# Output projection in seven block products per pair of sequences, with the sums of y made in the heads and kept in memory

## The chip, the cores and the metric

The kernel runs on one core of a Trainium2 chip. The metric is the device time of one execution in microseconds (us). One execution was also profiled, instruction by instruction. Engines: PE is TensorE, PEld its weight loads, DVE is VectorE, ACT is ScalarE, POOL is GpSimd, and SP is SyncE, which here issues nearly all DMA transfers, in program order.

## The reference

Four sequences of 512 tokens, 512 features; 16 heads of 128; a router over 64 experts. All in float32.

```python
def reference(x, slope_rate, w_qkv, w_gate, w_out, norm_w, router_weight, router_bias, expert_bias):
    xn = layernorm(x)
    # lightning attention on xn: per head a decayed causal attention
    q, k, v = split(silu(xn @ w_qkv.T))              # 16 heads of 128
    out = decayed_causal_attention(q, k, v, slope_rate)
    var = mean(out * out, -1)                        # over all 16 heads
    out = norm_w * (out * rsqrt(var + 1e-6))
    gate = sigmoid(xn @ w_gate.T)
    s = (gate * out) @ w_out.T                       # the output projection
    # router: top 8 of 64 by softmax
    scores = softmax(xn @ router_weight.T + router_bias)
    topk_w, topk_idx = top_k(scores, 8)
    f = xn * sum(topk_w) + sum(topk_w * expert_bias[topk_idx])
    return x + s * silu(f)
```

## The kernel before

PE multiplies float32 through a split: each operand becomes a high part (a cast to float32r, made on ScalarE by `split_hi`, L99) and a low part (the operand minus the high part, made by `split_lo`, L102, on VectorE or GpSimd). A product is then three passes (`PASSES`, L27): high by high, high by low and low by high.

The four sequences form two pairs (`PB` = 2, p = 0 and 1), the 16 heads eight groups of two (`GH`, `NG`). The kernel has three stages. The order of all instructions is written out by hand; Tile adds only the waits.

1. *Preparation and v* (to 186 us): layer norm, transposes, the router's logits, and v for all tokens, which goes to device memory.

2. *Heads* (to 863 us). The list `todo` has 24 units per pair: for each group a gate unit (`gate_unit`) and two units for q and k (`qk_unit`). Each unit is computed by `unit` (L484) in the Winograd form of a 2 by 2 block product: seven products instead of eight (`PRODUCTS`, L39), here with two sequences as one side's blocks and two weight matrices as the other's. A product is six matmuls of 128 x 512. Its result leaves its PSUM bank through an `add` on VectorE, or a copy on ScalarE. Between the products stand the lists `after[0]` to `after[6]`: the work of other steps that is issued after that product. There are the splits of the next unit's weights (on GpSimd), the attention of the head whose q and k were ready before (`attention`: scores in `after[1]`, states in `after[3]`, `attend` in `after[6]`), and in pair 0 the router's selection (`route_steps`). A gate unit has the attention of the group before's second head, the first q and k unit has none, the second has that of the first head. `attend` (L690) multiplies by the norm's weight and the gate and stores y, one tile of 128 x 512 per sequence and head (its features by the tokens), to `y_d`.

3. *Output projection* (from 863 us). `steps` goes over the four sequences and the 16 heads: 64 steps. `ahead` loads y (`load_y`) up to six steps ahead and splits it (`split_y`: high part on ScalarE, low part on VectorE) up to three ahead; in the first sequence it also loads w_o and splits it (`split_wo`, low part on GpSimd). A step is `o_head`: four token tiles by three passes, 12 matmuls with y as the weights of the array and 512 columns of w_o streamed, summed over 16 heads in four PSUM banks. At head 15 `finish` (L791) multiplies by the root mean square and by the gate of the experts, adds x and stores. Between the steps stand the last head's attention (`last_steps`), the sums of squares, and the experts' part (`ffn`, `silu_gate`). The last three heads of the last sequence are taken tile by tile, so that the finishing of a tile lies beside the next one's matmuls.

The last unit holds the start of stage 3:

```python
if i == len(todo) - 1:
    ahead(0, 2, 0)                       # loads of two y
    def more():
        ...
        ahead(0, 4, 1)                   # first split
    after[3].append(more)
    after[4].append(lambda: ahead(0, 4, 2))   # second split
    after[5].append(lambda: load_eb(op))
    after[6].append(lambda: ahead(0, 6, 2))
```

SBUF is handed out by pools. A tile with `bufs=n` shares n buffers with the others of its tag: the next tile waits until all that use the old one, DMA transfers too, are done.

Of the kernel before, what the change touches and what calls it, by code (L numbers as in the profile page):

```python
# [50 lines left out]
def kernel(  # L51
# [50 lines left out]
    def split_lo(eng, lo, src, hi):  # L102
# [31 lines left out]
    }  # L134
    y_d = {
        (b, h): dram.tile([P, N], F32, tag=f"y{b}_{h}", name=f"y_{b}_{h}")
        for b in range(B) for h in range(NH)
    }

# [47 lines left out]
    NX = 3  # L187
# [27 lines left out]
    def load_x(stage, b, t):  # L215
        xt = stage.tile([P, F], F32, tag="x", name=f"x_{b}_{t}")
        nc.sync.dma_start(out=xt, in_=x[tok(b, t), :])
        xts[b, t] = xt
# [470 lines left out]

    def attend(b, h, attp, psum=(ps_o, "o")):  # L690
# [7 lines left out]
        y = attp.tile([P, N], F32, tag="y", name=f"y_{b}_{h}")  # L698
        nc.vector.scalar_tensor_tensor(y, po, nw[:, h : h + 1], gts[s], ALU.mult, ALU.mult)  # L699
        nc.sync.dma_start(out=y_d[s], in_=y)  # L700
# [30 lines left out]
    def load_eb(outp):  # L731
        ebs.append(outp.tile([P, F], F32, tag="woin", name="raw_eb"))
        nc.sync.dma_start(out=ebs[0][0:E, :], in_=expert_b)
        nc.sync.dma_start(out=ebs[0][E : 2 * E, :], in_=expert_b)
# [12 lines left out]
    def ffn(b, t, outp):  # L747
        u = outp.tile([P, F], F32, tag="u", name=f"u_{b}_{t}")
        normalise(u, xts[b, t], b, t)
        pu = ps_sc.tile([P, F], F32, tag="sc", name=f"pu_{b}_{t}")  # L750
        for i in range(2):
            nc.tensor.matmul(pu, wT[b][:, t, :], ebs[0][:, i, :], start=(i == 0), stop=(i == 1))  # L752
        gates[b, t] = u, pu
# [7 lines left out]
    op = late = None  # L761
    wos = {}

    def load_y(b, h, op):
        y = op.tile([P, N], F32, tag="yin", name=f"yin_{b}_{h}")
        nc.sync.dma_start(out=y, in_=y_d[b, h])
        return y

    def split_y(b, h, op, y):
        yr = op.tile([P, 2, N], F32R, tag="yr", name=f"yr_{b}_{h}")  # L770
# [4 lines left out]
    def load_wo(h, op):  # L775
        w = op.tile([P, F], F32, tag="woin", name=f"woin_{h}")
        nc.sync.dma_start(out=w, in_=w_o[h // GH][:, h % GH, :])
        return w


    def split_wo(h, w):
        pool_, tag = (op, f"wr{h}") if h < 4 else (xa, f"x{h - 4}") if h < 4 + NX else (late, f"wr{h}")
        wr = pool_.tile([P, 2, F], F32R, tag=tag, name=f"wr_{h}", bufs=1)
        split_hi(wr[:, 0], w)
        split_lo(nc.gpsimd, wr[:, 1], w, wr[:, 0])
        wos[h] = wr
# [4 lines left out]
    def finish(b, t, ps, c=slice(None)):  # L791
        u, xt = gates[b, t][:, c], xts[b, t][:, c]
        last = b == B - 1
        nc.vector.scalar_tensor_tensor(u, ps[:, c], rms[b][:, t : t + 1], u, ALU.mult, ALU.mult)  # L794
        (nc.vector if last else nc.gpsimd).tensor_tensor(u, u, xt, ALU.add)  # L795

        def store():
            (nc.scalar if last and t % 2 else nc.sync).dma_start(out=out[tok(b, t), c], in_=u)
        if last:
            store()  # L800
        else:
            stores.append(store)


    def o_head(pos, h, yr, t, c=slice(None), stops=(NH - 1,)):
        for n, (wi, yi) in enumerate(PASSES):
            nc.tensor.matmul(  # L807
                pos[t][:, c], yr[:, yi, bass.ts(t, P)], wos[h][:, wi, c],
                start=(h == 0 and n == 0), stop=(h in stops and n == len(PASSES) - 1),
                skip_group_check=c != slice(None),  # L810
            )
# [184 lines left out]
    xc = op2 = None  # L996
    xc_stack = ExitStack()
    steps = [(b, h) for b in range(B) for h in range(NH)]
    parts, ys, ow = [], [], []
# [3 lines left out]
    def ahead(i, loads, splits):  # L1003
        nonlocal nload, nsplit
        while nload < min(i + loads, len(steps)):
            b, h = steps[nload]
            from_ = op if nload < 2 else op2
            ys.append(load_y(b, h, from_))
            if b == 0:
                ow.append(load_wo(h, from_))  # L1010
            nload += 1
        while nsplit < min(i + splits, len(steps)):
            b, h = steps[nsplit]
            from_ = op if nsplit < 2 else op2
            parts.append(split_y(b, h, from_, ys.pop(0)))
            if b == 0:
                split_wo(h, ow.pop(0))
# [9 lines left out]
    for i, (p, kind, n, w) in enumerate(todo):  # L1027
# [18 lines left out]
        if nu - len(XN) + NX <= i < nu:  # L1046
# [5 lines left out]
            load_block(1, m)  # L1052
        if i == nu - 1:
            for m in range(NX):
                def again(m=m):
                    block(1, len(XN) - NX + m, xa, m)
                    load_block(1, len(XN) - NX + m)
                after[m].append(again)
        if i == nu:
            xb_stack.close()  # L1060
            op = left(o_stack, "o", 2)
        if i == len(todo) - 1:
            ahead(0, 2, 0)


            def more():
                nonlocal op2
                xc_stack.close()
                op2 = left(o_stack, "o2", 4)
                ahead(0, 4, 1)  # L1070
            after[3].append(more)
            after[4].append(lambda: ahead(0, 4, 2))
            after[5].append(lambda: load_eb(op))
# [22 lines left out]
    pos = {}  # L1096
    for f in later:
        f()
    for i, (b, h) in enumerate(steps):
        last = b == B - 1  # L1100
        if i == len(last_steps):
            ha_stack.close()
            hw_stack.close()
            late = right(late_stack, "late", 5)

        if h < NH - 1:
            ahead(i, 6, 3)
            while stores:
                stores.pop(0)()
        if h == 0:  # L1110
            for t in range(NT):
                pos[t] = ps_mm.tile([P, F], F32, tag="mm", name=f"po_{b}_{t}")
        if not last or h < NH - TAIL:
            yr = parts.pop(0)
            for t in range(NT):
# [74 lines left out]
```

## Time and profile before

| | |
|---|---|
| time, median of 3 runs | 1060.59 us (1059.93 to 1064.33) |
| the profiled execution's own time | 1060.44 us |
| its span, first to last instruction | 1058.6 us |
| granted TensorE clock | 0.999 |
| PE busy from 0 to 863 us (v and heads) | 860.96 us |
| PE busy from 863 to 1000 us (projection) | 137.00 us |
| VectorE busy, 0 to 863 and 863 to 900 us | 419.91 and 22.04 us |
| GpSimd busy, 0 to 863 and 863 to 900 us | 613.77 and 25.56 us |
| DMA, whole execution | 143.09 MB, 135 GB/s |
| DMA share and rate, 863 to 900 us | 0.66, 220 GB/s |

How to read it: the page of the profile gives busy time by engine, the chain of work that ended last, and groups of instructions; a group's line has source line, engine, operation, tiles (written <- read), shape, count, then busy us, mean ns of one, and the idle time of its engine just before, with the work that ended most of it. The timeline lists instructions in order of time, merged where equal ones follow each other. A matmul's own duration includes its way through the array, so matmuls overlap: their price is the interval from start to start. Time is counted from the start of the span.

### The profile page before, as it was taken

How to read it: one execution, taken by the hardware profiler on the slowest of the kernel's cores; microseconds unless marked ns; L12 is line 12 of the kernel's file. 1: busy time of each engine (PE TensorE's matmuls, PEld its weight loads, DVE VectorE, ACT ScalarE, POOL GpSimd, SP SyncE). 2: the span in 40 equal slices, each digit the busy share in tenths (PEclk: the TensorE clock that was granted, in tenths of full speed). 3: DMA queues.
4: the chain of work that ended last, by engine and by line, in shares of the span. 5: the costliest groups of instructions: out<-in, count | busy, mean ns of one | idle time of the engine just before them, and what ended most of it. 6: DMA issues, size and time to landing. Idle time of an engine off the chain costs nothing.

```text
span 1058.6 us, 16166 instructions
## 1 busy us (share of the span) xinstructions
PE 1051.8 (99%) x5771; PEld 910.6 (86%) x5771; DVE 520.8 (49%) x869; ACT 520.5 (49%) x955; POOL 663.6 (63%) x694
## 2 busy tenths in 40 slices
PE   9999999999999999999999999999999999999998
PEld 8888888888888888888888888888888888888886
DVE  6666543355454545444444444444444456745354
ACT  5555555655555555555555555554555543332221
POOL 5888782857777678677785777767867756402020
PEclk9999999999999999999999999999999999999999
DMA  7456737422422233235722242232322546445351
GB/s 245 165 199 245 266 142 238 150 85 86 140 85 95 89 98 114 85 125 174 279 85 66 88 126 85 85 110 83 107 65 86 159 131 217 140 159 173 96 189 50
DMA packets 109872, 143.09 MB, mean 135 GB/s; under 512 B 9680, under 2 KB 58208, under 8 KB 108896
## 3 DMA queue, kind: packets, MB, share of 16 engines
q1 hardware_dynamic: 108752, 141.35, 40.8%
q8 instruction: 46, 0.75, 0.3%
q10 hardware_dynamic: 1040, 0.71, 0.2%
q14 instruction: 34, 0.28, 0.1%
HBM read 93.24 MB, written 50.87 MB: 136 GB/s over the span
## 4 chain that ended last, share of the span: by engine, by line
PE 98%; DVE 1%; DMA 0%; ACT 0%; POOL 0%; issue 0%; SPq 0%; ACTq 0%
PE u_qk L502 29%; PE po L807 16%; PE u_g L502 14%; PE u_v L502 13%; PE o L695 5%; PE sa L658 5%; PE o L697 4%; PE ss L681 4%; PE kt L661 2%; PE d_v L532 2%; PE lg L318 1%; PE pu L752 1%; PE pt L251 1%; DMA x<-in_x_dram 0%; PE ssq L724 0%; ACT w_A_v L100 0%
## 5 line engine op out<-in xcount | busy, mean ns | idle before, releaser
L807 PE MATMUL po<-wr,yr 128*128 128x512 f32 (+1 forms) x777 | 178.7, 388 | 0.9 <-DVE u L794 0.9
L807 PEld LDWEIGHTS po<-wr,yr 128*128 128x128 f32 x777 | 144.4, 188 | 30.4 <-DVE u L794 1.1
L502 PE MATMUL u_qk<-blk_T,ws_qk 128*128 128x512 f32 x576 | 146.9, 395 | 0.0
L707 POOL TENSOR_TENSOR sqs<-sqs,sq 128x512 f32<-128x512 f32 x60 | 77.8, 1296 | 76.3 <-ACT sq L706 76.3
L502 PEld LDWEIGHTS u_qk<-blk_T,ws_qk 128*128 128x128 f32 x576 | 105.8, 188 | 20.2
L103 POOL TENSOR_TENSOR ws_qk<-sum_qk,ws_qk 128x512 fp32r<-128x512 f32 x64 | 82.8, 1295 | 40.6 <-ACT ws_qk L100 39.6
L502 PE MATMUL u_qk<-blk_B,wa_qk 128*128 128x512 f32 x384 | 99.1, 394 | 0.0
L695 PE MATMUL o<-at,vin 128*128 128x128 f32 x512 | 88.4, 275 | 0.0
L502 PEld LDWEIGHTS u_qk<-blk_B,wa_qk 128*128 128x128 f32 x384 | 71.0, 188 | 14.1
L103 DVE TENSOR_TENSOR yr<-yin,yr 128x512 fp32r<-128x512 f32 x64 | 60.6, 960 | 44.3 <-ACT yr L100 44.1
L103 POOL TENSOR_TENSOR ws_g<-sum_g,ws_g 128x512 fp32r<-128x512 f32 x32 | 41.3, 1290 | 59.1 <-ACT ws_g L100 59.1
L695 PEld LDWEIGHTS o<-at,vin 128*128 128x128 f32 x512 | 75.0, 192 | 2.5
L502 PE MATMUL u_g<-blk_T,ws_g 128*128 128x512 f32 x288 | 76.0, 400 | 0.0
L667 ACT ACTIVATE kd<-kt,kdecay 128x384 f32<-128x384 f32 x64 | 37.2, 582 | 77.8 <-PE kt L661 77.8
L699 DVE SCALAR_TENSOR_TENSOR y<-o,nw,gt 128x512 f32<-128x512 f32 x64 | 48.0, 751 | 55.1 <-PE o L697 55.1
L697 PE MATMUL o<-qd,st 128*128 128x128 f32 x384 | 74.3, 275 | 0.0
L706 ACT ACTIVATE sq<-o 128x512 f32<-128x512 f32 x60 | 35.9, 598 | 75.1 <-POOL sqs L707 42.3
L685 DVE SCALAR_TENSOR_TENSOR st<-st,bdecay,ss 128x128 f32<-128x128 f32 x128 | 41.7, 346 | 59.0 <-ACT st L683 56.8
L795 POOL TENSOR_TENSOR u<-u,x 128x512 f32<-128x512 f32 x12 | 17.8, 1517 | 84.0 <-DVE u L794 84.0
L100 ACT CAST yr<-yin 128x512 fp32r<-128x512 f32 x64 | 39.2, 617 | 63.0 <-PE po L807 39.4
L546 ACT ACTIVATE k<-k 128x512 f32<-128x512 f32 x64 | 40.4, 632 | 57.4 <-DVE k L493 57.4
L658 PE MATMUL sa<-q,k 128*128 128x128 f32 x512 | 67.5, 275 | 0.0
(180 smaller groups left out, 2295.7 us busy)
## 6 DMA issues: line engine op xcount, KB each, us to landing
v<-vo_v SPq DMA_DIRECT2D x64, 256.0 KB, 2.7
raw_qk<-in_w_head_dram SPq DMA_DIRECT2D x64, 256.0 KB, 3.7
vin<-v SPq DMA_DIRECT2D x64, 256.0 KB, 3.6
y<-y SPq DMA_DIRECT2D x64, 256.0 KB, 2.1
yin<-y SPq DMA_DIRECT2D x64, 256.0 KB, 2.8
x<-in_x_dram SPq DMA_DIRECT2D x32, 256.0 KB, 4.3
raw_g<-in_w_head_dram SPq DMA_DIRECT2D x32, 256.0 KB, 3.2
raw_v<-in_w_v_dram SPq DMA_DIRECT2D x16, 256.0 KB, 5.9
```

Source lines behind the costliest of these rows:

```text
L100: nc.scalar.copy(hi, src)
L103: eng.tensor_tensor(lo, src, hi.bitcast(F32), ALU.subtract)
L502: nc.tensor.matmul(ps, lhsT, rhs, start=(first and c == 0 and n == 0), stop=(c == KC - 1 and n == len(PASSES) - 1), skip_group_check=not f ...
L546: nc.scalar.activation(dst, src, AF.Silu)
L658: nc.tensor.matmul(pa[:, c], k[:, c], q[:, c], start=True, stop=True)
L681: nc.tensor.matmul(ps[:, c], kd[s][:, c], v_of(b, h, c), start=True, stop=True)
L685: nc.vector.scalar_tensor_tensor(r[:, c], r[:, c - 1], bdecay[:, h : h + 1], ps[:, c], ALU.mult, ALU.add)
L695: nc.tensor.matmul(o, v_of(b, h, c), at[s][:, c], start=True, stop=(c == 0))
L697: nc.tensor.matmul(o, st[s][:, c - 1], qd[s][:, c - 1], start=False, stop=True)
L699: nc.vector.scalar_tensor_tensor(y, po, nw[:, h : h + 1], gts[s], ALU.mult, ALU.mult)
L707: nc.gpsimd.tensor_tensor(sq[b], sq[b], s1, ALU.add)
L807: nc.tensor.matmul(pos[t][:, c], yr[:, yi, bass.ts(t, P)], wos[h][:, wi, c], start=(h == 0 and n == 0), stop=(h in stops and n == len(PASS ...
```

## The change

The output projection takes the form that the units of the heads already have. Per pair of sequences, y is a matrix of blocks: A11 and A12 are the first sequence's y of the even and of the odd head of a group, A21 and A22 the second sequence's. w_o has the blocks B11 to B22: even or odd head, first or second half (`H2` = 256) of the output features. For each pair the seven products of `PRODUCTS` are taken in turn, each summed over the eight groups: `steps` now has 2 x 7 x 8 = 112 steps, each of 12 matmuls of 256 columns (`o_group`). Three accumulators of two PSUM banks each (`accs`) hold them, and `o_sums` combines the products: 0 is copied on ScalarE, 1 and 2 are added on VectorE, product 3 gives the first quarter of the result, 4, 5 and 6 the others; `finish` works on halves of 256 columns.

The sums of y that the products need (S1 to S4) are made on VectorE in the heads (`keep_y`, run from the list `ysums` in steps 1, 3 and 5 of a later unit) and kept in `y_d`, as are A11, A12 and A22. The sums of w_o (T1 to T4) are made once, in eight units in the middle of pair 0 (`sum_wo`, in steps 3 to 6), and kept in `wo_d`. In the projection w_o is loaded product by product and split there; products 3 and 6 are loaded and split again for pair 1. The first products' w_o is split during pair 1's heads. `NX` goes from 3 to 4.

```diff
     y_d = {
-        (b, h): dram.tile([P, N], F32, tag=f"y{b}_{h}", name=f"y_{b}_{h}")
-        for b in range(B) for h in range(NH)
+        (p, m, q): dram.tile([P, 2, N], F32, tag=f"y{p}_{m}_{q}", name=f"y_{p}_{m}_{q}")
+        for p in range(B // PB) for m in range(NM) for q in range(NQ)
     }
+    wo_d = [dram.tile([P, NM, NQ, H2], F32, tag=f"wo{j}", name=f"wo_{j}") for j in range(2)]
...
+    def keep_y(b, h, y, attp):
+        p, g = b // PB, h // GH
+        n = f"A{b % PB + 1}{h % GH + 1}"
+        yb[n] = y
+        def store(n):
+            nc.sync.dma_start(out=y_d[p, AN.index(n), g // 2][:, g % 2], in_=yb[n])
+        def sum_of(n, a, b, op):
+            yb[n] = attp.tile([P, N], F32, tag="ysum", name=f"y{n}_{p}_{g}", bufs=3)
+            nc.vector.tensor_tensor(yb[n], yb[a], yb[b], op)
+            store(n)
+        if n in AN:
+            store(n)
+        for last, *what in (
+            ("A11", "S3", "A11", "A21", ALU.subtract), ("A12", "S1", "A21", "A22", ALU.add),
+            ("A12", "S2", "S1", "A11", ALU.subtract), ("A12", "S4", "A12", "S2", ALU.subtract),
+        ):
+            if n == last:
+                ysums.append(lambda what=what: sum_of(*what))
+
+    def sum_wo(g, stage):
+        w = stage.tile([P, NM + 1, H2], F32, tag="wo", name=f"wosum_{g}", bufs=1)
+        of = {n: w[:, i] for i, n in enumerate(BN + ["B12"])}
+        for n in ("B11", "B12", "B21", "B22"):
+            k, j = int(n[1]) - 1, int(n[2]) - 1
+            nc.sync.dma_start(out=of[n], in_=w_o[g][:, k, bass.ts(j, H2)])
+        def sum_of(n, a, b):
+            nc.vector.tensor_tensor(of[n], of[a], of[b], ALU.subtract)
+            if n == "T4":
+                nc.sync.dma_start(out=wo_d[g // NQ][:, :, g % NQ], in_=w[:, 0:NM])
+        sums = ("T1", "B12", "B11"), ("T2", "B22", "T1"), ("T3", "B22", "B12"), ("T4", "B21", "T2")
+        return [lambda a=a: sum_of(*a) for a in sums]
...
+        wr = pool_.tile([P, 2, NQ, H2], F32R, tag=tag, name=f"wr_{m}_{j}", bufs=1)
         split_hi(wr[:, 0], w)
-        split_lo(nc.gpsimd, wr[:, 1], w, wr[:, 0])
-        wos[h] = wr
+        for i in range(2):
+            c = bass.ts(i, NQ // 2)
+            split_lo(nc.gpsimd, wr[:, 1, c], w[:, c], wr[:, 0, c])
+        wos[m, j] = wr
...
+    def finish(b, t, src, j, m, last):
+        u, xt, c = gates[b, t], xts[b, t], bass.ts(j, H2)
+        tail_ = last and m == NM - 1
+        nc.vector.scalar_tensor_tensor(u[:, c], src, rms[b][:, t : t + 1], u[:, c], ALU.mult, ALU.mult)
+        (nc.vector if tail_ else nc.gpsimd).tensor_tensor(u[:, c], u[:, c], xt[:, c], ALU.add)
...
+    def o_sums(p, m, x, ps, ts, last):
...
+        def add(dst, what, i=slice(0, 2)):
+            nc.vector.tensor_tensor(dst[:, i], ps[:, i], ochain[what, x][:, i], ALU.add)
+        s1 = (wk, "s1", 1) if x == 0 else (late, "s1b", 1)
+        if m == 0:
+            nc.scalar.copy(temp("s1", *s1), ps)
+        elif m == 1:
+            add(temp("a", wk, "a", 2), "s1")
+        elif m == 2:
+            add(temp("e", wk, *(("e", 1) if x == 0 else ("sqs", 2))), "a")
+        else:
+            i2, j2 = ((0, 0), (1, 1), (0, 1), (1, 0))[m - 3]
+            dst = (lambda: ps, lambda: ochain["e", x], lambda: temp("c", *s1), lambda: ochain["a", x])[m - 3]()
+            for i in ts:
+                if m > 3:
+                    add(dst, "e" if m == 4 else "a", slice(i, i + 1))
+                finish(b0 + i2, 2 * x + i, dst[:, i], j2, m, last)
...
+        if 0 <= i - nu // 2 < NG:
+            for j, f in enumerate(sum_wo(i - nu // 2, again)):
+                after[3 + j].append(f)
+        for j in (1, 3, 5):
+            if ysums:
+                after[j].append(ysums.pop(0))
...
         if i == len(todo) - 1:
-            ahead(0, 2, 0)
             def more():
...
-                op2 = left(o_stack, "o2", 4)
-                ahead(0, 4, 1)
+                op2 = left(o_stack, "o2", 2)
+                ahead(0, 6, 0)
             after[3].append(more)
-            after[4].append(lambda: ahead(0, 4, 2))
-            after[5].append(lambda: load_eb(op))
             after[6].append(lambda: ahead(0, 6, 2))
...
+    def o_group(acc, m, g, yr, t):
+        first = PRODUCTS[m][3]
+        for n, (wi, yi) in enumerate(PASSES):
+            nc.tensor.matmul(
+                acc[t // 2][:, t % 2], yr[:, yi, bass.ts(t, P)], wos[m, g // NQ][:, wi, g % NQ],
+                start=(first and g == 0 and n == 0 and t % 2 == 0), stop=(g == NG - 1 and n == len(PASSES) - 1),
+                skip_group_check=True,
+            )
...
+    for i, (p, m, g) in enumerate(steps):
+        last = p == NP - 1
+        if i == 6:
+            while ysums:
+                ysums.pop(0)()
...
+        ahead(i, (8, 9, 8, 7, 6, 7, 8)[i] if i < 7 else 10, 4)
...
+        for b, t in tiles_at.get(i - 1, ()):
+            silu_gate(b, t)
+        yr = parts.pop(0)
...
+            for t in range(NT):
+                o_group(acc, m, g, yr, t)
+            if g == NG - 1:
+                for j in range(2):
+                    o_sums(p, m, j, acc[j], (0, 1), last)
...
+        for b, t in tiles_at.get(i, ()):
+            ffn(b, t, late)
```

## The prediction

> **What bounds the kernel now.** I read the page first, then the TensorE (PE) timeline of the projection and of the heads, then VectorE (DVE) and GpSimd (POOL) beside it. The profiled execution took 1060.44 us: a span of 1058.6 and 1.84 outside it, 0.15 under the median of the three runs (1060.59), so I count from 1060.4. From the page:
>
> ```profile
> PE 1051.8 (99%) x5771; PEld 910.6 (86%) x5771; DVE 520.8 (49%) x869; ACT 520.5 (49%) x955; POOL 663.6 (63%) x694
> PE 98%; DVE 1%; DMA 0%; ACT 0%; POOL 0%; issue 0%; SPq 0%; ACTq 0%
> L103 DVE TENSOR_TENSOR yr<-yin,yr 128x512 fp32r<-128x512 f32 x64 | 60.6, 960 | 44.3 <-ACT yr L100 44.1
> ```
>
> PE is 98% of the chain that ended last, the other engines have room on average. So PE time removed is time gained, and any new PE wait is time lost, in full. The third line is the work on which the projection hangs: VectorE's low half of each y. Two stretches of the PE timeline give the price of a matmul:
>
> ```profile
> 974.01 5.60 PE L807 MATMUL po<-wr,yr 128*128 128x512 f32 x24
> 1053.77 1.00 PE L807 MATMUL po<-wr,yr 128*128 128x256 f32 x7
> ```
>
> Columns: start, length, line, count. Less one matmul's own duration (0.39 and 0.28 us, from the groups by form) over one interval fewer than the count: 0.2265 us per 512 columns, 0.120 per 256. Half the columns cost 53%, not 50%.
>
> **The gain.** Removed: 759 products of 512 columns and 18 of 256, 171.9 + 2.2 = 174.1 us. Added: 2 pairs x 7 products x 8 groups x 4 token tiles x 3 passes = 1344 products of 256 columns, 161.3 us. PE gains 12.8 us, not the eighth of 174 (21.8) that seven products for eight promise.
>
> [...]
>
> **Start of the projection: +4.0 us.** Before, the first two low halves of y are made in the last unit, ahead of the last attention's y. After, loads only come after product 3, and both first splits stand in `after[6]`, behind that attention. The third split of before stood in just that place:
>
> ```profile
> 863.30 0.75 DVE L699 SCALAR_TENSOR_TENSOR y<-o,nw,gt 128x512 f32<-128x512 f32 x1 [0.81 <-PE o L697]
> 865.67 1.37 DVE L103 TENSOR_TENSOR yr<-yin,yr 128x512 fp32r<-128x512 f32 x1 [1.62 <-ACT yr L100]
> ```
>
> It waited for ScalarE's cast, which stood behind a square that waited for POOL, and ended at 867.04. PE reached the projection at 863.02 and nothing else is queued there: 4.0 us (3.5 if the split meets no POOL work, 6 if loads are late too). [...]
>
> **The sums of w_o: +7.5 us.** Eight units of pair 0 each load four blocks of w_o, subtract on VectorE from step 3 on, and store seven; the tile has one buffer. So the next unit's loads, on SP, wait until the last store has landed, and VectorE's first subtraction, T1, waits for them in its queue, with the sum of product 4 behind it. PE cannot start product 6 on that bank before that sum. The places, in a unit without attention that starts at 624.62:
>
> ```profile
> 624.90 0.75 DVE L699 SCALAR_TENSOR_TENSOR y<-o,nw,gt 128x512 f32<-128x512 f32 x1 [0.81 <-PE o L697]
> 631.71 0.69 DVE L493 TENSOR_TENSOR k<-u_qk,e_qk 128x512 f32<-128x512 f32 x1 [2.03 <-PE u_qk L502]
> 632.88 1.52 PE L502 MATMUL u_qk<-blk_T,wb_qk 128*128 128x512 f32 x6
> ```
>
> With U the start: the last T4 ends at U+1.5 (y, then 0.42 for 256 columns). The store of 896 KB: 256 KB take 2.1 us and 512 KB 3.4, so an estimate of 5.3, landing at U+7.2. Two 128 KB loads (2.6 us each, issued 0.4 apart) make U+10.2, T1 and the sum U+11.3; product 6 is due at U+8.3. That is 3.0 us, in the three such units (13, 16, 19). In units with attention T1's place is U+11, after the states, and it costs 0 to 0.4. If the store lands as a small one does, 2 us sooner, 1.0 each remains. I take 2.5 x 3; bounds 0 and 10.5.
>
> The other additions to the heads I cost at nothing: 64 sums of y on VectorE (0.69 us, up to 1.8 beside POOL) stand three in each unit that has no attention, where VectorE idles about 2 us per product, and one after `at`; without that cover each would delay an eviction by up to 1 us. 48 more y stores meet DMA engines 20 to 40% busy.
>
> **VectorE in the projection: +11 us.** A step now lasts 12 x 0.120 = 1.44 us, not 2.72, and still needs one split of y. Alone it takes 0.69; beside POOL this is what happens:
>
> ```profile
> 897.50 1.77 DVE L103 TENSOR_TENSOR yr<-yin,yr 128x512 fp32r<-128x512 f32 x1
> 902.22 0.69 DVE L103 TENSOR_TENSOR yr<-yin,yr 128x512 fp32r<-128x512 f32 x1 [1.21 <-ACT yr L100]
> 885.05 6.58 POOL L103 TENSOR_TENSOR wr<-woin,wr 128x512 fp32r<-128x512 f32 x4
> ```
>
> The first ran while POOL split a weight, the second while POOL idled; the third row has POOL's splits at 1.6 us each where alone they take 1.29. Sums that read PSUM stay at 0.69. So each POOL operation of 512 columns costs VectorE about 1.05 us where they meet, and six products of pair 0 and two of pair 1 have four of them: 4.2 us.
>
> VectorE's demand per product against PE's 96 x 0.120 = 11.5 us, each with 8 splits = 5.5: Products 1 and 2 of pair 0 add two evictions (1.4), 4.2, and three and four token tiles (normalise 0.54, gate 0.74): 15.0 and 16.3, against 12.9 and 13.3 with the router matmuls on PE. Products 3 and 4: 11.8 and 11.6. Product 5 carries the finish of product 4: four sums of 256 columns (0.43), four multiplies (0.48), three waits of 0.31 for POOL's additions (0.74), and 4.2: 14.2. Product 0 of pair 1 has that finish and four tiles: 15.2 against 13.3. Product 5 of pair 1: 14.2. The excesses 2.1 + 3.0 + 0.3 + 0.1 + 2.7 + 1.9 + 2.7 make 12.8. At step 6 four sums of y come at once in front of a split due in three steps (4.3 us): they take 2.8 to 6, so +2. The lead of three splits absorbs about 2 per pair: -4. That leaves 11. Bounds: 3, if POOL's work mostly falls between splits, and 20, if every finish of products 4, 5, 6 (4.6 us in order ahead of the next split) is exposed as well.
>
> **Tail: +1.4 us.** After the last matmul a sum (0.43) is added. The four tiles need 4 x 1.4 us of VectorE behind 3 x 1.08 of PE: 2.3 us after the last matmul where before it was 0.9. Bounds 0.5 and 2.3.
>
> ScalarE gets 112 casts of 0.62, 16 of weights at twice that and 16 silus of 0.63, 99 of some 180 us: room. The projection moves about 48 MB in 175 us, 275 GB/s; the stretch from 863 to 900 had 220 GB/s at a share of 0.66, so 333 at most: covered, with little over. Where SP waits for a split before it may load y, the stores of out behind it are not urgent. A weight's POOL splits are due a product later.
>
> **Sum.** -12.8 + 4.0 + 7.5 + 11 + 1.4 = +11.1: 1060.4 + 11.1 = 1071.5 us.
>
> **Rivals.**
> A, faster: VectorE's lead covers the projection but for the finishing chains (1), and the w_o tiles arrive in time (0). The place is the three splits of lead; it decides if a product's demand stays under 11.5 us. -12.8 + 4.0 + 1 + 1 = -6.8: 1053.6. For it: VectorE is 49% busy and idled 44.3 us before splits. Against: the 1.77 rows. Chance 0.17.
> B, even: w_o costs one stall (2.5), VectorE 6: -12.8 + 4.0 + 2.5 + 6 + 1.4 = +1.1, 1061.5. Chance 0.18.
> C, the products of 256 are no cheaper: weight loads bound them. PEld's own duration is 188 ns, and the nine of the last half took 1.34 us, 0.132 each with the start. At 0.132 the new work is 177.4 us, a loss of 3.3 where I have a gain of 12.8: 1087.6. Against: seven in a row at 0.120. [...] Chance 0.08.
> The forecast has 0.57.
>
> **How the numbers follow.** A measurement of this kernel tells about 0.5% (5.3 us) from no change. Low end: A's time, 1053.6, a little below the sum of the best bounds (-12.8 + 3.5 + 0 + 3 + 0.5 = -5.8, 1054.6). High end: 7.5 + 20 + 4 + 1.4 - 12.8 = +20, plus half of C's distance (8), 1088. The range 1053.6 to 1088 leaves out half of A and half of C. The forecast's own range is 1066 to 1083. Faster 0.17 (A), same 0.18 (B), slower 0.65 (forecast and C).
>
> **What would show it.** PE: 1344 products of 256 columns, 0.120 apart where dense. Right on the start: a PE gap of about 4 us before the first product, ended by `yr`. Right on w_o: VectorE waiting for a DMA of w_o in units 13, 16, 19, and PE waiting 2 to 3 us before product 6 there. Right on VectorE: over 85% busy in the projection, splits averaging above 1 us, PE idle time ended by `yr`, mostly after products 4 to 6 and in tiles' steps. Wrong: PE dense from the heads to the tail (then 1048 to 1050), an interval above 0.125 us, or PE waiting for `yin` or `woin` transfers rather than for VectorE.

## The result, and the profile after

The changed kernel takes 1096.62 us (median of 4 runs, 1092.85 to 1099.64) against 1061.75 for the kernel before on the same chip: 1.0325 times as long, 95% interval 1.0283 to 1.0367. Slower, as forecast, but by 35 us where 11 were forecast, and above the range (1053.6 to 1088). The profiled execution took 1099.64 us, span 1097.7: the slowest of its runs, 39.1 us more than the span before.

The page of the kernel after, engines and the two groups of the new work:

```profile
PE 1058.5 (96%) x6338; PEld 935.3 (85%) x6338; DVE 646.6 (59%) x1059; ACT 556.7 (51%) x1009; POOL 726.8 (66%) x730
L1185 PE MATMUL acc<-wr,yr 128*128 128x256 f32 x1344 | 174.0, 288 | 10.3 <-DVE yr L103 6.6
L103 DVE TENSOR_TENSOR yr<-yin,yr 128x512 fp32r<-128x512 f32 x112 | 104.1, 969 | 33.7 <-ACT yr L100 33.6
```

PE fell from 99 to 96% busy: idle time rose from 7 to 39 us. The count of 1344 is as announced, and where the products run dense their interval is 0.120 us (the median): the price of the gain was right. Table by stretch (us, busy time and count of PE, PEld, DVE, ACT, POOL, granted clock, DMA share, GB/s):

```profile
350.00:500.00 150.00, 136.28 (x772) 116.97 (x771) 86.90 (x167) 69.24 (x127) 99.89 (x98) 0.97 0.57 176
500.00:884.00 384.00, 384.00 (x2267) 338.91 (x2266) 199.73 (x317) 203.00 (x367) 290.98 (x284) 1.00 0.42 138
884.00:900.00 16.00, 12.59 (x83) 12.20 (x82) 9.06 (x10) 6.83 (x12) 5.63 (x5) 0.79 0.24 82
950.00:1000.00 50.00, 46.33 (x368) 44.35 (x367) 45.84 (x56) 24.89 (x40) 30.40 (x24) 1.00 0.71 243
1000.00:1050.00 50.00, 47.93 (x364) 45.04 (x363) 38.52 (x58) 23.48 (x41) 9.74 (x8) 1.00 0.69 245
```

The 384 us in the middle are full. The loss lies in two places: 350 to 500 us, the units that make the sums of w_o, and the projection from 884. In both the granted clock (the third number from the right), which before was 1.00 until the tail, is below 1. PE's waits over the whole execution (waited for: us in total, times, longest):

```profile
PE u_qk L506 <- DVE k L497: 11.2, 4, 3.4
PE acc L1185 <- DVE yr L103: 6.6, 6, 2.3
PE pu L798 <- DVE u L803: 3.5, 6, 1.1
PE acc L1185 <- ACT yr L100: 2.4, 1, 2.4
PE u_g L506 <- DVE gt L497: 2.4, 3, 1.4
PE pu L798 <- DMA wTin<-wTd: 2.3, 1, 2.3
```

The first and fifth line are the sums of w_o (forecast 7.5 in all), the second and fourth splits of y. The third and the last, the router's product `pu`, were in no step of the prediction. Unit 13, on PE, VectorE and SP:

```profile
376.62 1.52 PE L506 MATMUL u_qk<-blk_B,ws_qk 128*128 128x512 f32 x6
381.54 2.93 PE L506 MATMUL u_qk<-blk_T,wb_qk 128*128 128x512 f32 x6 [3.40 <-DVE k L497]
```

```profile
379.86 0.43 DVE L730 TENSOR_TENSOR wosum<-wosum 128x256 f32<-128x256 f32 x1 [3.91 <-DMA wosum<-in_w_o_dram]
380.20 0.69 DVE L710 TENSOR_TENSOR yS<-yS,y 128x512 f32<-128x512 f32 x1
380.80 0.69 DVE L497 TENSOR_TENSOR k<-u_qk,e_qk 128x512 f32<-128x512 f32 x1
```

```profile
371.53 0.89 SPq L732 DMA_DIRECT2D wo<-wosum  x1
372.47 1.76 SPq L422 DMA_DIRECT2D raw_g<-in_w_head_dram  x2
377.09 1.75 SPq L727 DMA_DIRECT2D wosum<-in_w_o_dram  x4
```

The store goes out at 371.53, the loads into the same buffer at 377.09, T1 at 379.86, and the sum of product 4, which frees the bank of product 6, only then. The forecast mechanism is there. But between T1 and that sum stands a sum of y, which the prediction had put at nothing, and the six matmuls behind the gap take 2.93 us where the six before it took 1.52: half clock (the granted clock was 0.50 from 380.10 to 386.93 us).

### The profile page after: what moved, and what is told of

It reads as the page before. It is cut to its first block, busy times and chain, and to the rows that moved or that the text cites. A ratio compares the mean times of both kernels' runs of the same rounds, so it can differ in the third digit from the quotient of the medians.

```text
span 1097.7 us, 17793 instructions
## 1 busy us (share of the span) xinstructions
PE 1058.5 (96%) x6338; PEld 935.3 (85%) x6338; DVE 646.6 (59%) x1059; ACT 556.7 (51%) x1009; POOL 726.8 (66%) x730
## 5 line engine op out<-in xcount | busy, mean ns | idle before, releaser
L1185 PE MATMUL acc<-wr,yr 128*128 128x256 f32 x1344 | 174.0, 288 | 10.3 <-DVE yr L103 6.6
L1185 PEld LDWEIGHTS acc<-wr,yr 128*128 128x128 f32 x1344 | 168.3, 195 | 16.5 <-DVE yr L103 10.3
L103 DVE TENSOR_TENSOR yr<-yin,yr 128x512 fp32r<-128x512 f32 x112 | 104.1, 969 | 33.7 <-ACT yr L100 33.6
L506 PEld LDWEIGHTS u_qk<-blk_T,ws_qk 128*128 128x128 f32 x576 | 105.9, 188 | 20.5
L103 POOL TENSOR_TENSOR ws_qk<-sum_qk,ws_qk 128x512 fp32r<-128x512 f32 x64 | 88.4, 1390 | 46.2 <-ACT ws_qk L100 46.2
L506 PE MATMUL u_qk<-blk_B,wa_qk 128*128 128x512 f32 x384 | 101.3, 400 | 0.0
L103 POOL TENSOR_TENSOR wr<-woin,wr 128x512 fp32r<-128x512 f32 x36 | 54.8, 1548 | 65.5 <-ACT wr L100 63.0
L100 ACT CAST yr<-yin 128x512 fp32r<-128x512 f32 x112 | 65.8, 616 | 51.0 <-PE acc L1185 29.1
L673 POOL TENSOR_TENSOR qd<-q,dec 128x384 f32<-128x384 f32 x64 | 70.2, 1117 | 0.0
```

The lines of the kernel that those rows point to most:

```text
L100: nc.scalar.copy(hi, src)
L103: eng.tensor_tensor(lo, src, hi.bitcast(F32), ALU.subtract)
L506: nc.tensor.matmul(ps, lhsT, rhs, start=(first and c == 0 and n == 0), stop=(c == KC - 1 and n == len(PASSES) - 1), skip_group_check=not f ...
L673: nc.gpsimd.tensor_tensor(qd[s], q[:, 1:], d[:, 1, None, :].to_broadcast([P, NT - 1, P]), ALU.mult)
L1185: nc.tensor.matmul(acc[t // 2][:, t % 2], yr[:, yi, bass.ts(t, P)], wos[m, g // NQ][:, wi, g % NQ], start=(first and g == 0 and n == 0 and ...
```

## The experiments

### The wait for w_o: two links in series

`wo2`: a second buffer, nothing else.

```diff
-        w = stage.tile([P, NM + 1, H2], F32, tag="wo", name=f"wosum_{g}", bufs=1)
+        w = stage.tile([P, NM + 1, H2], F32, tag="wo", name=f"wosum_{g}", bufs=2)
```

> One change to the changed kernel: the tile in which the sums of w_o are made has two buffers instead of one. Theory (the reload waits for the store): the six PE gaps between 377 and 482 us (14.2 us together) and the half clock behind two of them (6.8 and 3.4 us long, so 5.1 us of work) go; 1096.6 becomes about 1077, and VectorE's idle time ended by the DMA of w_o falls from 15.0 us to under 2. Rival (the added VectorE work in these units crowds out the evictions, whatever the loads do): the subtractions and the sums of y stay, so at most 3 us are won, 1093 or more.

Measured 1094.18 us, ratio 1.0321 (1.0301 to 1.0340): a miss, 2.4 us in place of some 20. Even these are not clear of the spread: the changed kernel's own ratio is 1.0325 (1.0283 to 1.0367), and run again (`a_base` below) it took 1099.02. SP's waits in the kernel after held the first line below; in `wo2` it is gone, and still the loads leave late and T1 waits (the other lines: SP and VectorE of `wo2`, unit 13):

```profile
SPq L727 <- DMA wo<-wosum: 9.7, 7, 3.1
```

```profile
366.54 1.88 SPq L706 DMA_DIRECT2D y<-y  x2
371.40 2.49 SPq L727 DMA_DIRECT2D wosum<-in_w_o_dram  x4
376.58 0.42 DVE L730 TENSOR_TENSOR wosum<-wosum 128x256 f32<-128x256 f32 x1 [3.25 <-DMA wosum<-in_w_o_dram]
```

SP issues in order, and ahead of these loads stand the stores of y (first of the two SP lines) that the unit before queued, which wait for that unit's last attention. The three long gaps, 3.3 to 3.6 us in the kernel after, are still 2.9 us each: taking away one of two waits in series gave little.

`woahead`: two buffers, and the four loads issued one unit earlier (`sum_wo` cut into `load_wsum` and `sum_wo`).

```diff
-            for j, f in enumerate(sum_wo(i - nu // 2, again)):
+            for j, f in enumerate(sum_wo(i - nu // 2)):
...
+        if 0 <= i + 1 - nu // 2 < NG:
+            load_wsum(i + 1 - nu // 2, again)
```

> Two buffers for the sums of w_o as in the run before, and their loads stand one unit earlier in SP's order. With two buffers alone the loads were issued only at 371.4 us, behind the last unit's stores of y (which wait for y until 368.1), the store of the sums and two weight loads, and landed at 376.1, so 3 us of PE gap stayed. Theory (it is the place in SP's queue, not the buffer alone): VectorE's wait for these loads ends before 1 us, the gaps between 375 and 480 us and their half clock (about 19 us together) go: 1075 to 1077. Rival (the subtractions themselves, 0.42 to 0.87 us ahead of the evictions, or the transfers of 896 KB, hold PE): 8 us or more of it stays, 1083 or more.

1082.04 us, ratio 1.0207 (1.0188 to 1.0225): 12.1 us under `wo2`, 14.6 under the kernel after; the place in SP's queue is the larger link, though 1075 to 1077 had been expected. PE is busy for 146.92 of the 150 us from 350 to 500, against 136.28. One gap of 2.7 us stays, in unit 16: there VectorE has a step of the router's selection, T1 and a sum of y ahead of the sum of product 4, and beside GpSimd T1 takes 1.51 us (0.42 alone) and the sum of y 1.75 (0.69 alone):

```profile
422.56 1.51 DVE L736 TENSOR_TENSOR wosum<-wosum 128x256 f32<-128x256 f32 x1
423.99 1.75 DVE L710 TENSOR_TENSOR yS<-yS,y 128x512 f32<-128x512 f32 x1
```

### The start of the projection, and VectorE beside GpSimd

Three kernels on top of `wo2`. `wo2early` moves the first splits ahead of the last attention, `wo2early_actlo` also writes a plain cast of w_o, made on ScalarE, where its low part belongs, and so leaves the low part out of the result; `wo2early_dvelo` makes the low part on VectorE.

```diff
-            after[6].append(lambda: ahead(0, 6, 2))
+            after[6].insert(0, lambda: ahead(0, 6, 2))
...
-            split_lo(nc.gpsimd, wr[:, 1, c], w[:, c], wr[:, 0, c])
+            split_hi(wr[:, 1, c], w[:, c])                        # wo2early_actlo
+            split_lo(nc.vector, wr[:, 1, c], w[:, c], wr[:, 0, c])  # wo2early_dvelo
```

> As the kernel with two buffers, and the first two splits of y stand ahead of the last attention in step 6 of the last unit. Theory (the splits stand behind the attention's squares): the gap of 3.8 us at the start of the projection and the 6.8 us of half clock behind it (3.4 us of work) go; 7 us less than the kernel with two buffers alone, about 1070. Rival (the loads of y, issued only after step 3, come too late): the casts wait for the DMA instead, and 0 to 2 us are won, 1075 to 1077.

1091.12 us, ratio 1.0286 (1.0268 to 1.0303): 3.1 us less instead of 7. The gap at the start is gone; waits of 0.9, 1.1 and 1.3 us between 903 and 913 came in its place, and the granted clock from 860 to 1070 us is 0.98 as in `wo2`. And in the heads, where the edit changes nothing, the profiled execution had a clock of 0.94 from 350 to 500 us against 0.97 in that of `wo2`.

> As the kernel before it in this list, but the low part of w_o is written by a copy on ScalarE in place of GpSimd's subtraction; the output's low part is left out thereby. It takes GpSimd's weight splits out of the projection. Theory (VectorE and GpSimd hold each other up): the mean split of y falls from 0.97 to under 0.8 us, VectorE's busy time in the projection from 160 to about 130 us, and PE's idle time there to a few us: 10 to 14 us less than with the two repairs alone, about 1058. Rival (VectorE has too many operations whatever GpSimd does, or the loads of y come late): under 4 us less.

1079.73 us, ratio 1.0181 (1.0166 to 1.0196): 11.4 less than `wo2early`, as expected, and the mean split of y falls to 761 ns.

> As the kernel with the two repairs, but the low part of w_o is made on VectorE instead of GpSimd: 32 more subtractions of 512 columns on VectorE (22 us at 0.69), none on GpSimd. Theory (a GpSimd operation costs VectorE 1.05 us where they meet, its own subtraction 0.69): a little less than with the two repairs, 0 to 5 us. Rival (VectorE is bound by the number of its operations): up to 15 us more.

1084.55 us, ratio 1.0224 (1.0208 to 1.0239): 6.6 less than `wo2early`, more than the 0 to 5 expected, although VectorE now does 32 operations more. The splits of y in `wo2early`, then in `wo2early_dvelo`:

```profile
L103 DVE TENSOR_TENSOR yr<-yin,yr 128x512 fp32r<-128x512 f32 x112 | 105.5, 984 | 33.4 <-ACT yr L100 33.4
```

```profile
L103 DVE TENSOR_TENSOR yr<-yin,yr 128x512 fp32r<-128x512 f32 x112 | 81.2, 760 | 32.1 <-ACT yr L100 32.0
L103 DVE TENSOR_TENSOR wr<-woin,wr 128x512 fp32r<-128x512 f32 x32 | 20.6, 684 | 0.9 <-ACT wr L100 0.9
```

The work of GpSimd was costing VectorE 24 us on the splits (105.5 against 81.2), more than the 20.6 that VectorE needs to do it itself. In the trace of the kernel after, the 34 splits of y beside which GpSimd did nothing took at most 0.69 us; the 78 that ran beside its work took 1.09 in the mean, up to 1.79. Its sums that read PSUM and one SBUF tile (`o_sums`) took 0.42 us at 256 columns and 0.68 at 512, beside GpSimd's work as without it.

### A ring through four engines

`fix1`: `woahead` and `wo2early_dvelo` together, and the router products of pair 0 three steps later.

```diff
-            tiles_at.setdefault((10, NM * NG + 1)[b // PB] + 8 * (b % PB) + 2 * t, []).append((b, t))
+            tiles_at.setdefault((13, NM * NG + 1)[b // PB] + 8 * (b % PB) + 2 * t, []).append((b, t))
```

> The kernel above with the first splits ahead of the last attention, the low part of w_o on VectorE, and the router's steps of pair 0 three projection steps later (13 instead of 10), so that its weights, held up on SP behind the four last sums of y, land in time. The two first were worth 3 and 6.6 us before; the third removes a wait of 1.9 to 2.7 us and 1.7 us of half clock behind it. Theory: the parts add up, 1076 - 3 - 6.6 - 4 = 1062. Rival (the projection is bound by VectorE's total, so a repaired wait comes back at the next place): 1066 or more.

1074.04 us, ratio 1.0129 (1.0113 to 1.0145): 12 above expectation, where the rival had put it (1066 or more). Its PE waits in the projection are led by this line, and the timeline (VectorE, ScalarE, PE) shows one such wait:

```profile
PE pu L804 <- DVE u L809: 8.2, 7, 1.6
```

```profile
905.16 0.74 DVE L809 SCALAR_TENSOR_TENSOR u<-u,sumw,pu 128x512 f32<-128x512 f32 x1
907.10 0.69 DVE L103 TENSOR_TENSOR yr<-yin,yr 128x512 fp32r<-128x512 f32 x1 [1.21 <-ACT yr L100]
```

```profile
905.93 0.63 ACT L810 ACTIVATE u<-u 128x512 f32<-128x512 f32 x1 [3.13 <-DVE u L809]
906.47 1.12 ACT L100 CAST yr<-yin 128x512 fp32r<-128x512 f32 x2
```

```profile
910.76 0.73 PE L804 MATMUL pu<-ebs,wTin 128*128 128x512 f32 x2 [1.22 <-DVE u L809]
```

ScalarE waits 3.13 us for VectorE's gate sum (L809) before its silu (L810), though the casts queued behind the silu had nothing to wait for. VectorE then waits 1.21 us for such a cast, and its next gate sum, for which PE waits, comes late. No engine is full (from 900 to 950 us PE is busy for 43.25 us, VectorE for 39.83, ScalarE for 27.22); each waits for the next in turn.

`fix2` gives the splits a longer lead, `fix3` also moves the last four sums of y to GpSimd.

```diff
-        ahead(i, (8, 9, 8, 7, 6, 7, 8)[i] if i < 7 else 10, 4)
+        ahead(i, (8, 9, 8, 7, 6, 7, 8)[i] if i < 7 else 10, 6)   # fix2
...
-            nc.vector.tensor_tensor(yb[n], yb[a], yb[b], op)
+            eng.tensor_tensor(yb[n], yb[a], yb[b], op)           # fix3
```

> As the kernel above, with splits of y issued up to five steps ahead of PE instead of three. Theory (the finishing chains of products 4 to 6, 4.6 us in order, overrun a lead of 4.3 us): a lead of 7.2 us covers them, 2 to 5 us less. Rival (the six buffers of split y and the late loads of y set the lead, not the order): no change within 1.5 us.

> As the kernel above, with the four last sums of y (at step 6 of the projection) on GpSimd, which is then nearly idle there, instead of VectorE. Theory (their burst stands ahead of the split due next): 1 to 2 us less. Rival (GpSimd takes 1.3 us or more for each and holds VectorE's splits up, and SP's stores wait longer): the same or 1 to 3 us more.

1086.15 us (ratio 1.0240, 1.0214 to 1.0266) and 1088.23 (1.0271, 1.0255 to 1.0287): both worse than `fix1`, `fix2` by 12 us where 2 to 5 less were expected; that `fix3` lies 2.1 above `fix2` is not clear of the spread. With more splits queued in front of the gate sum, the wait of `pu` for it grew from 8.2 to 12.0 us in `fix2`, and the sum of squares waited 5.5.

`gate` keeps the lead of `fix1` and opens the ring: the gate sum goes ahead of the step's splits, the silu one step later, when its input is long there. `gate_only` makes the same edit in the changed kernel as it is.

```diff
-        nc.scalar.activation(u, u, AF.Silu)
...
+        for b, t in tiles_at.get(i - 1, ()):
+            silu_gate(b, t)
         ahead(i, (8, 9, 8, 7, 6, 7, 8)[i] if i < 7 else 10, 4)
...
-        for b, t in tiles_at.get(i - 1, ()):
-            silu_gate(b, t)
+        for b, t in tiles_at.get(i - 2, ()):
+            nc.scalar.activation(gates[b, t], gates[b, t], AF.Silu)
```

> As fix1, but in a projection step the router's sum on VectorE stands ahead of the next split of y, and its silu on ScalarE one step later, behind the casts. In fix1 PE waits 8.2 us in seven places for that sum before the next router matmul, and VectorE waits 1.21 us each time for a cast that stands behind the silu. Theory (a ring of sum, silu, cast and split, 4.8 us per two steps against 3.65 of PE, and not VectorE's busy time): those waits go, 7 to 9 us less than fix1, about 1066. Rival (VectorE's total): less than 3 us, since the wait returns at the splits.

> The changed kernel with one edit: the router's sum ahead of the split of y, its silu one step later. Theory (the ring of sum, silu, cast and split holds PE by itself): PE's waits for that sum (3.5 us, 6.8 with those put down to the weight loads) and the stretch of the ring go, 5 to 10 us less than the changed kernel, 1087 to 1092. Rival (in the changed kernel VectorE's contention with GpSimd bounds the same stretch, the ring only shows once that is gone): less than 3 us.

`gate`: 1062.11 us (10 runs), ratio 1.0018 (1.0005 to 1.0032), 11.9 less than `fix1`, more than the 7 to 9 expected. `gate_only`: 1086.09, ratio 1.0243 (1.0224 to 1.0262), 10.5 less than the kernel after. So of the changed kernel's loss some 10 us are this ring, with not one operation added or removed. The edit moves the gate sum and the silu together; which of the two moves counts for how much is not shown. In `gate_only` the wait is down to the first line, and a stretch that had 47.93 us of PE work is full:

```profile
PE pu L798 <- DVE u L803: 0.7, 2, 0.5
```

```profile
1000.00:1050.00 50.00, 50.00 (x409) 49.47 (x408) 38.25 (x55) 26.32 (x45) 10.15 (x8) 1.00 0.73 241
```

### Is half clock a price of its own?

So far gaps and half clock went together. `a_base` is the changed kernel again. `a_warm_heads` computes product 4 of units 13, 16 and 19 three times into its own bank; nothing that PE waits for is moved, PE only has 8.2 us more to do. `a_warm_all` also has 27 needless matmuls ahead of the projection and 18 ahead of the first `pu`.

```diff
-            for c in range(KC):
+            times = 3 if i == 4 and name in ("qk_0_8", "qk_0_10", "qk_0_12") else 1
+            for c in [c for _ in range(times) for c in range(KC)]:
...
+        if i == 0:
+            warm(acc[0].rearrange("p t w -> p (t w)"), 27, 0)   # a_warm_all
```

> The changed kernel again, as the reference for the two beside it: about 1096 us, with gaps of 3.3 to 3.6 us in units 13, 16 and 19 and half clock behind most of the gaps over 2.3 us.

> In units 13, 16 and 19 product 4 is computed three times into its own bank: 36 matmuls of 512 columns more, 8.2 us of added TensorE work, in front of the wait for the sum of product 4. No wait is removed. Theory (an idle gap over about 2.3 us costs its length and then half clock for 3.4 or 6.8 us more): the work fits into the gaps, which shrink to 0.6 to 0.9 us, no half clock follows there, and the time falls by 3 to 5 us although there is more to do. Rival (the clock falls for another reason, or the half clock is no price of its own): same time within 1 us, or up to 8 more if the work isn't hidden.

> As a_warm_heads, and 27 needless matmuls of 256 columns ahead of the projection's first product and 18 ahead of the first router product, each into a bank that the next real matmul overwrites: 5.4 us of work in the two gaps of the projection behind which the clock was halved (6.8 and 3.4 us). Theory: another 4 to 5 us less than a_warm_heads, some 8 to 10 under a_base, and the granted clock at 1.00 from 300 us to the tail. Rival: the same as a_warm_heads or more.

`a_base` 1099.02 us, ratio 1.0358 (1.0337 to 1.0379); `a_warm_heads` 1093.70, ratio 1.0304 (1.0287 to 1.0321): 5.3 us less with 8.2 us more work. In unit 13 product 6 starts at the same time in both, 380.52 and 380.60 us. Two stretches of `a_base`, then of `a_warm_heads`; the clock is the third number from the right:

```profile
370.00:395.00 25.00, 21.62 (x102) 17.98 (x101) 12.73 (x19) 11.04 (x20) 16.46 (x18) 0.86 0.73 223
425.00:450.00 25.00, 21.47 (x102) 17.83 (x101) 14.82 (x28) 9.33 (x19) 15.82 (x16) 0.86 0.64 196
```

```profile
370.00:395.00 25.00, 24.12 (x125) 19.92 (x124) 14.28 (x27) 11.11 (x21) 17.28 (x18) 1.00 0.77 237
425.00:450.00 25.00, 23.07 (x133) 19.59 (x132) 14.33 (x27) 9.58 (x19) 15.31 (x15) 1.00 0.54 165
```

That is a price of the half clock alone in the heads: the waits were left, the idleness was not. It belongs to a clock of 0.86, 0.86 and 0.93 in the 25 us from 370, from 425 and from 475 us of `a_base`'s profiled execution, against 1.00 in all three in that of `a_warm_heads`; the kernel after had 0.86, 1.00 and 0.93 there. The second part is a miss: `a_warm_all`, 1092.73 (1.0294, 1.0276 to 1.0312), gained 1 us more, which is not clear of the spread, not 4 to 5. From 880 to 900 us the clock rose from 0.83 to 1.00, but PE reached the first router products earlier than their inputs: its waits for `pu` grew from 2.3 to 4.5 us for VectorE, and the clock from 900 to 925 us was still 0.93 (0.86 in `a_warm_heads`).

### All repairs together

`fix4`, on `gate`: the subtractions of w_o in `after[2]`, `[4]`, `[5]`, `[6]`, and the sums of squares and the split of the expert bias some steps later. `fix5`: `fix4` with a lead of four splits.

```diff
-                after[3 + j].append(f)
+                after[(2, 4, 5, 6)[j]].append(f)
...
-        if i in (8, 10):
-            sum_squares((b0, b1)[i // 2 - 4])
+        if i in (12, 14):
+            sum_squares((b0, b1)[i // 2 - 6])
...
+        ahead(i, (8, 9, 8, 7, 6, 7, 8)[i] if i < 7 else 10, 5)   # fix5
```

> As gate, and three more places: the subtractions of w_o one after each of steps 2, 4, 5, 6 (in unit 16 the first stood with a router step and a sum of y in one place, PE gap 2.7 us and 1.7 us of half clock), the sums of squares four steps later (PE gap 1.1 us, 3.4 us long half clock behind it), the split of the experts three steps later (ScalarE stood 3.9 us before a DMA). Theory: 2.7 + 1.7 + 1.1 + 1.7 = 7 us less than gate, about 1059, level with the kernel before. Rival (these gaps only move): 3 us less or none.

> As fix4, with the splits of y four steps ahead instead of three. In the earlier run a lead of five cost 12 us, because the router's sums stood behind the splits; now they stand ahead. Theory (a lead covers the finishing chains of products 4 to 6 once nothing waits behind it): 1 to 3 us less than fix4. Rival (the six buffers of split y make VectorE wait for PE in order, ahead of everything else): the same or more.

1062.68 us (1.0032, 1.0015 to 1.0050) and 1064.51 (1.0040, 1.0025 to 1.0055), where 7 us less than `gate` and 1 to 3 less again were expected: neither helped. Unit 16's gap was still 2.7 us: a router step and a sum of y still stood ahead of the eviction.

`fix6`, on `gate`: the order that these gaps ask for. Nothing is computed that `gate` does not compute; only the low part of w_o for product 0, made during the heads, goes back from VectorE to GpSimd.

```diff
-            split_lo(nc.vector, wr[:, 1, c], w[:, c], wr[:, 0, c])
+            split_lo(nc.vector if m else nc.gpsimd, wr[:, 1, c], w[:, c], wr[:, 0, c])
...
-                after[3 + j].append(f)
+                after[(4, 5, 6, 6)[j]].append(f)
...
-        for j in (1, 3, 5):
+        for j in (1, 4, 5):
...
-            tiles_at.setdefault((13, NM * NG + 1)[b // PB] + 8 * (b % PB) + 2 * t, []).append((b, t))
+            tiles_at.setdefault((13, NM * NG + 4)[b // PB] + 8 * (b % PB) + 2 * t, []).append((b, t))
...
+        if i == 2:
+            ysums.pop(0)()
...
-                for t in range(NT):
+                for t in (0, 2, 1, 3):
```

(and the later sums of squares and expert bias of `fix4`.)

> The kernel gate with the waits that its trace still shows taken out one by one: the subtractions of w_o and a sum of y after steps 4 to 6, where no eviction is due (2.7 us and 1.7 of half clock in unit 16); the last tiles in the order 0, 2, 1, 3, so that a tile's sum does not hold the PSUM bank that the next one fills (1.6 us); the first products' w_o split on GpSimd in the heads (0.9 us); sums of squares and the experts' split later, one of the four last sums of y earlier (2.5 us); the router's steps of pair 1 three steps later (0.6 us). Theory: 1062 - 9 = 1053, with PE dense in the projection; that is faster than the kernel before. Rival (VectorE, 48 of 50 us busy at 900 to 950, and the DMA queues at 0.84 return the waits elsewhere): 1058 to 1062.

1055.18 us (5 runs, 1054.76 to 1057.37) against 1060.56 of before: ratio 0.9949 (0.9937 to 0.9962). This beats both kernels, that of before by 5.4 us (half a per cent) and the changed one by some 41. Its parts were not run one by one, so what each of them is worth is not shown. Two stretches of it, and PE's longest waits from 300 us on:

```profile
350.00:500.00 150.00, 149.34 (x880) 130.61 (x879) 104.05 (x181) 79.17 (x146) 114.54 (x111) 1.00 0.62 196
900.00:950.00 50.00, 49.90 (x403) 48.99 (x402) 48.46 (x82) 30.09 (x49) 9.06 (x9) 1.00 0.81 288
```

```profile
PE acc L1192 <- DVE yr L103: 1.8, 2, 1.4
PE pu L804 <- DMA wTin<-wTd: 0.9, 1, 0.9
```

In the second stretch VectorE is busy for 48.46 of 50 us and PE still for 49.90: the amount of VectorE work is not what bounds the projection here, with GpSimd's splits of w_o gone from it.

## Why the prediction was wrong, step by step

Of the 39.1 us between the two spans, about 2.5 lie in the first 25 us, which the change does not touch and in which executions differ (from 0 to 186 us PE was busy for 181.29 us in the kernel after, for 184.53 in `wo2early_dvelo`). The rest, by the intervals between PE's instructions:

| step | forecast | in the profile after |
|---|---|---|
| PE's gain | -12.8 | 0.120 us per product: -12.8 |
| start of the projection | +4.0 | gaps of 2.55 and 1.29: 3.8 |
| sums of w_o | +7.5 | gaps of 3.6, 3.3 and 3.4, and 4.0 in units 15, 17, 18: 14.2 |
| half clock | not in the sum | 20.5 us at half, in part beside the gaps; matmuls longer by 4.2 in the heads and 4.1 in the projection |
| VectorE in the projection | +11 | waits for splits 6.1, for the router 6.5, and 9.2 in 66 stalls of 0.05 to 0.5 |
| tail | +1.4 | two waits for a sum, 1.6, where before there was one of 0.95; 0.5 more behind the last matmul: 1.1 |

The rows and the first 25 us add up to 38.9 us.

**Right:** the sign; the price of a product; the place and size of the start's gap; units 13, 16 and 19 as the places of the long stalls; GpSimd as the cause of long splits; the size of the tail. Rival C, and with it the fear that the weight loads bound the products, fell: 0.120 held.

**The term "the sums of w_o: +7.5" was mis-sized,** at 14.2 before the clock, above its bound of 10.5. The sum of y behind T1 was one of the additions "at nothing", and its cover, VectorE's idle time, was gone just where T1 waited. The units with attention, put at 0 to 0.4, lost 4.0 in all. And the cause was half of it: `wo2` shows that the buffer alone is worth 2.4 us at most, `woahead` that loads queued on SP behind stores that wait are the other link, with 12.1 us.

**The half clock was not in the sum.** In the trace before, PE's longest wait after the first 2 us is 0.9 us and the granted clock is 1.00 from 5.3 to 1056.6, so nothing there shows what a stall of 2.5 or 4 us does to it, and the forecast put no price on it, neither at the start nor at the three 2.5 us stalls that it forecast itself. In the kernel after it took 4.2 us in the heads and 4.1 in the projection, and `a_warm_heads` confirms by a run that it has a price of its own there: 5.3 us.

**"VectorE in the projection: +11" had the wrong kind of working,** and measured 21.8, of which 2.4 is the router's load below. It summed VectorE's demand per product against PE's 11.5 us. The average was not the limit: in `fix6`, where GpSimd splits no w_o beside it, PE is full (49.90) with VectorE busy for 48.46 of 50 us. In the kernel after VectorE was not over 85% busy as announced, but 163.5 of the projection's 214 us (76%), with splits of 0.97 us in the mean, not above 1. What was missing is the order: gate sum, silu, cast, split and gate sum again, worth 10.5 us (`gate_only`). The step that put ScalarE's silus down as "room" is the one that failed: room it had, but its queue stood still 3 us at a time. GpSimd's share was as forecast in kind, and 6.6 to 11.4 us in size (the 11.4 with the low part of w_o left out) once the other waits were partly open.

**The router's load** of `wTin`, behind stores of y on SP that wait for the burst of sums at step 6, cost 2.3 us and was named nowhere; the text only called the stores of out not urgent.

Rival A's time, 1053.6, is what the repaired order reaches (1055.18), and its condition was too loose: a product's demand under 11.5 us is not enough, the order in each queue must fit too.

Open: how much of GpSimd's contention and of the ring overlap in the kernel after, since the single repairs (14.6, 10.5, 6.6 to 11.4, 3.1) were measured on different bases; and why the first 25 us differ between executions.

## What to carry to other kernels

Where one engine is full and the others have room on average, price a change by the queues, not by busy shares: for each new operation write down what stands ahead of it and behind it on its engine and on SP, and follow the rings that cross several engines. A wait with two links shows almost nothing when one is cut (2.4 us in `wo2`), and a longer lead can be worse (12 us in `fix2`), since what runs ahead stands in front of what is due. Of the kernel after's six longest gaps on TensorE in the heads and the projection, 2.4 to 3.6 us, half clock followed four (last section), so such gaps were worth pricing at their length and at up to 1.7 or 3.4 us of half clock on top; needless matmuls in three of them paid 5.3 us (`a_warm_heads`).

## What the runs showed of the hardware

Between the first 200 us and the tail of the kernel after, half clock came in stretches of 3.41 or 6.83 us, so it cost up to 1.7 or 3.4 us of work where PE had work to do. There it followed gaps of 3.57 (6.83), 3.42 (3.41), 2.55 and 1.29 with one matmul between (6.83), and 2.41 us (3.41); it did not follow 3.28 and 2.43, while in `a_base` the clock around the place of the 3.28, from 425 to 450 us, was 0.86 against 1.00.

In the trace of the kernel after, half clock goes with the idle time within fixed pieces of time, not with the length of the gap. Its first record of the clock starts at 4.64 us, and each of the nine changes after it lies a whole multiple of 3.41333 us later, to 0.002 us. With PE's timeline from 200 to 1090 us cut at these multiples, PE was idle for 1.97, 2.27, 2.66 and 2.68 us in the four pieces at full clock that half clock followed, and for at most 1.83 us in each of the 249 others. The 3.28 us gap was cut in two at 431.30, with 1.83 us of idle time in the piece before the cut. `a_base`, the same kernel, had half clock around that place, so whether a gap is followed by half clock changes between two executions. The pieces are read off one trace; no run moved a gap against them to test it, and how little idle time is enough is not shown.

GpSimd beside VectorE cost more here than it took over: moving 32 splits to VectorE (`wo2early_dvelo`) shortened its other 112 from 984 to 760 ns each, 24.3 us for 20.6.
